# A graph layer's spilled edges summed in a free place of the last slot tile, and a re-ordered lead-in

## The chip, the cores and the metric

The kernel runs on one core of a Trainium2 chip. Its time is the device time of one execution in microseconds (us). The core has five engines with an instruction queue each: TensorE (PE, with its weight loads shown as PEld), VectorE (DVE), ScalarE (ACT), GpSimd (POOL) and SyncE (SP), which here only issues transfers. Each engine works through its instructions in the order in which they were written and waits at semaphores for the others.

## The reference, cut to what matters

```python
N, E, D = 6250, 100000, 128            # nodes, edges (sorted by dst), width
Xs  = x[src]
msg = where(edge_type == 0, Xs @ W_data.T + b_data, Xs @ W_control.T + b_control)
agg = segment_sum(msg, dst, N)
out = relu(agg + (x @ W_self.T + b_self))
return layernorm(x + out)              # over the 128 columns, eps 1e-5
```

Nodes are padded to 49 blocks of 128. Inputs and output are float32.

## The kernel before

**The table.** The message of an edge depends only on its source node and its type, so the kernel first computes one row for each of the 2 x 49 x 128 pairs. Each value is kept as three bfloat16 parts that add up to the float32 value, so a row has 3 x 128 columns. `multiply` computes a block of 128 nodes for both types on PE (`y`, lines 464 and 466), `take` copies a part to SBUF on ScalarE (`m`, line 475) and `leave` subtracts it again on PE (line 482), three parts in turn. All parts stay in SBUF (`m3`, 98 source tiles of 128 rows), and `store` also writes them to memory (`table`, line 492).

**Edges by destination block.** Edges are sorted by destination, so the edges of a block lie in a window of 18 x 128 edges. `starts` finds where the windows begin: an indirect load fetches 49 rows of edges (`er`), VectorE counts (`less`, `first_f`), PE turns the counts into one row (line 359), VectorE writes `first` (line 361), and SP then reads each start into a register and loads the window (`win`, line 376).

**Two ways to sum.** 40 blocks (the "p" blocks, eight groups of five) are summed with the table in SBUF. The other nine (the "g" blocks) fetch each edge's row from the table in memory by an indirect load on POOL (`msg`, line 845) and sum on PE (`agg_g`), in between the p blocks' work.

For a p block the edges are sorted into 98 buckets, one per source tile, of R = 32 places each:

- `edge_fields` (VectorE) splits the edges of a group into fields; `bucket_hots` compares them with the bucket numbers (`hot_st`, line 550).
- `ranks` gives each edge its place in its bucket, 18 steps a group: PE adds up `tri` times the hots (`acc`), VectorE takes the maximum (`slot`, line 567), PE adds `rest`. It is a chain between the two engines.
- `fill_a` and `fill_b` put the source row and the destination of each edge into its place (`two`, `v`, line 604).
- `fill_c` copies the result (`vs`), writes the source rows to memory (`packed`, line 622), turns the destinations into columns of four buckets each (`vd`, line 632; `to`, line 637), and lists the edges that found no place in their bucket, the spilled edges, at most 32 a group. Their positions in the list come from eight matmuls (lines 652 and 654), the list itself from a further eight (line 677), and POOL gathers their table rows (`msg_s`, line 694).
- `spread` loads `packed` to all 128 partitions (`rows`, line 718), `select` compares it with the partition number (line 725): a one-hot matrix that picks source rows.
- `gather` multiplies it with a source tile: 4 x 32 rows of messages, four buckets, a slot tile (`g_ps`, line 752). There are 25 slot tiles for 98 buckets; in the last one the buckets 96 and 97 fill half of the partitions, and its other two matmuls repeat bucket 97.
- `evict` copies the tile to SBUF as `gs` (line 761, ScalarE; in the last group VectorE too), `to_hots` builds the one-hot of destinations in two pieces per block (`hot_d`, line 739), and `add_up` multiplies the two into the block's sum `agg`. After the last tile one more set of matmuls adds the spilled edges (`msg_s` by `hot_s`). Row 32 of these tiles holds b_self and a row of ones, so that this also adds the bias; the g blocks have a pair of tiles for the bias alone (`msg_b`, `hot_b`).

Every sum is written as four matmuls of 32 output partitions each (`by_columns`, line 229):

```python
for c in range(0, P, 32):
    T.matmul(out[c : c + 32], lhsT[:, c : c + 32], rhs, **flags)
```

`own_of` adds `W_self x` to the sum in float32. `finish_blocks` adds the three parts (`whole`, line 150), applies relu and adds x; `normalise` does the layer norm for a whole group (root on ScalarE, `scale` on VectorE, one activation per block on ScalarE, line 187) and stores it. The group's sums use one PSUM buffer, so the next block's first sum waits for `whole`.

**The order.** All of these are Python generators of steps. A planner (`Order.run`) holds an assumed cost for each step and engine, a due time (`due`) and what the step needs, and picks which step comes next; the engines' instruction queues are written in that order. A changed cost or due time therefore moves instructions on every queue, and nothing else decides the order: the schedule isn't changed by the chip or the compiler.

Of the kernel before, what the change touches and what calls it, by code (L numbers as in the profile page):

```python
# [9 lines left out]
F32 = mybir.dt.float32  # L10
BF16 = mybir.dt.bfloat16
# [8 lines left out]
P = 128  # L20
# [23 lines left out]
NC = 4 * NS  # L44
XS = 4
RB = 3
M = 8
SLOT = 128.0
# [163 lines left out]
def sums_over_windows(ctx, tc, x, xt, edges, w, bias, table, packed, total,  # L212
# [42 lines left out]
    bias3 = const.tile([P, 2 * D], BF16, name="bias3")  # L255
# [16 lines left out]
    for i in range(3):  # L272
        A.copy(bias3[32 * i : 32 * i + 1, :], parts[0:1, i, : 2 * D])
# [6 lines left out]
    for j in range(RJ):  # L280
# [18 lines left out]
               for n in sorted({DC, CH, *GROUPS})}  # L299
# [3 lines left out]
    spill_tiles = [(const.tile([P, Q * P], BF16, name=f"hot_s{i}"),  # L303
                    const.tile([P, D3], BF16, name=f"msg_s{i}")) for i in range(2)]
    hot_b = const.tile([P, P], BF16, name="hot_b")
    msg_b = const.tile([P, D3], BF16, name="msg_b")
    slot_values = [const.tile([P, (Q + 1) // 2, NC], BF16, name=f"vs{i}") for i in range(2)]
    slot_b = {n: const.tile([P, R, n], BF16, name=f"slot{n}") for n in sorted({*GROUPS})}

    def constants():  # L310
# [13 lines left out]
        yield step("set2", {"V": 1.2})  # L324
# [3 lines left out]


        for vs in slot_values:  # L330
            V.memset(vs, 255.0)


        for i, (hot, msg) in enumerate([*spill_tiles, (hot_b, msg_b)]):
            yield step(("spill0", i), {"V": 1.6})
            V.memset(hot, 0.0)
            V.memset(hot[R : R + 1, :], 1.0)
            V.memset(msg, 0.0)
            V.tensor_copy(msg[R : R + 1, :].rearrange("p (i c) -> p i c", i=3),
                          parts[0:1, :, 2 * D :])  # L340
# [7 lines left out]
    def starts():  # L348
        yield step("er", {"S": 0.0}, lag=10.0)
# [12 lines left out]
        for b in [*range(STARTS[2]), *range(NPB, NB), *range(STARTS[2], NPB)]:  # L362
            grp = [g for g in range(NPG) if STARTS[g] <= b][-1] if b < NPB else NPG
            free = [("fields", grp - 2)] if 1 < grp < NPG else []
            yield step(("win", b), {"S": 0.84}, "first", *free, lag=2.0)
# [26 lines left out]
    def due(kind, *i):  # L392
        if kind in ("p", "g") and i[0] in ("root", "rooted", "scale", "apply", "out"):
            n = i[1] + 1
            return BUILT + 10 + (BLOCK * sum(GROUPS[:n]) if kind == "p" else PACE * KT * GQ * n)
# [15 lines left out]
        if kind in ("set2", "spill0"):  # L411
            return 40.0
# [3 lines left out]
        if kind == "table":  # L416
            return LEAD + each * (at_part[i[0]] + PARTS[i[0]]) + 6
# [39 lines left out]
    def multiply():  # L457
        for i, (g, b, n) in enumerate(two_blocks):
            for j in range(n):
# [6 lines left out]
                T.matmul(y[:, j, :], ones_b, bias3, start=False, stop=True, skip_group_check=True)  # L466
# [35 lines left out]
    places, spills, rows = {}, {}, {}  # L502
# [38 lines left out]
    def bucket_hots():  # L541
        chunks = [(grp, c) for grp in range(NPG) for c in range(KT // KC)]
        for i, (grp, c) in enumerate(chunks):
            n = GROUPS[grp]
            free = [("v", chunks[i - HB][0], chunks[i - HB][1] * KC + KC - 1)] if i >= HB else ["set"]
            yield step(("hot", grp, c), {"V": 0.13 + KC * NT * n / 1920}, ("fields", grp), ("counts", n), *free)
# [26 lines left out]
    def fill_a():  # L573
        for grp, n in enumerate(GROUPS):
            for c in range(KT // KC):
                yield step(("two", grp, c), {"V": 0.4 + 0.3 * n}, ("rank", grp, c * KC + KC - 1), ("slots", n),
# [32 lines left out]
    def fill_c():  # L609
        for grp, n in enumerate(GROUPS):  # L610
# [6 lines left out]
            A.copy(vs[:, : n // 2, :NT], vt[:, : n // 2, :])  # L617
            if n % 2:
                A.copy(vs[: 2 * R, n // 2, :NT], vt[: 2 * R, n // 2, :])
            yield step(("packed", grp), {"S": 0.4}, ("vs", grp), lag=2.5)  # L620
            for i in range(2):
                nc.sync.dma_start(
                    packed[b0 + i : b0 + n : 2, :].rearrange("j (r s) -> r j s", r=R),
                    vs[2 * R * i : 2 * R * i + R, : (n + 1 - i) // 2, :NT],
# [4 lines left out]
            for q in range(n):  # L629
                c0 = (q % 2 * 2 + 1) * R  # L630
                for t in range(4):
                    T.matmul(vd_v[t * R : (t + 1) * R, q, :], ident_b[:, c0 : c0 + R],
                             vs[:, q // 2, t::4], start=True, stop=True, skip_group_check=True)
            free = [("d", STARTS[grp - 1] - 1, (NS - 1) // DC)] if grp > 1 else []
            yield step(("to", grp), {"A": 0.3}, ("vd", grp), *free)
            to = work.tile([P, Q, NS], BF16, name="to")
            A.copy(to[:, :n, :], vd_v)
# [4 lines left out]
            yield step(("over", grp), {"V": 0.7}, ("rank", grp, KT - 1), ("to", grp))  # L642
# [5 lines left out]
            flags = work.tile([P, M], BF16, name="flags", bufs=1)  # L648
            V.tensor_single_scalar(flags, last, 0.0, op=ALU.is_gt)
            yield step(("pos", grp), {"T": 0.6}, ("over", grp), ("to", grp))  # L650
            pos = ps_a.tile([P, 512], F32, name="small")
            T.matmul(pos[:, :M], tri, flags, start=True, stop=False, skip_group_check=True)
            for c in range(M - 1):
                T.matmul(pos[:, c + 1 : M], ones_b,
                         flags[:, c : c + 1].to_broadcast([P, M - 1 - c]),
                         start=False, stop=c == M - 2, skip_group_check=True)
# [13 lines left out]
            V.tensor_copy(pos_sb, pos[:, :M])  # L670
# [5 lines left out]
            for c in range(M):  # L676
                T.matmul(listed[:R, :4], hs[:, c, :], f4[:, c, :], start=c == 0, stop=c == M - 1,
                         skip_group_check=True)
            free = [("sum", STARTS[grp - 1] - 1)] if grp > 1 else []
# [11 lines left out]
            hot_s, msg_s = spills[grp] = spill_tiles[grp % 2]  # L691
            V.tensor_scalar(hot_s[:R, : n * P], iota_f[:R, : n * P], dq, None, op0=ALU.is_equal)
            yield step(("spilled", grp), {"G": 0.8}, ("listed", grp), *stored, lag=2.5)
            G.indirect_dma_start(  # L694
                out=msg_s[:R], out_offset=None, in_=table[:, :],
# [25 lines left out]
    def select():  # L721

        for b in range(NPB):
            yield step(("sel", b), {"V": 1.2}, ("rows", b))
            V.tensor_scalar(rows[b], rows[b], pid1, None, op0=ALU.is_equal)  # L725

    def to_hots():
        tiles = [(b, c) for b in range(NPB) for c in range(-(-NS // DC))]
        for i, (b, c) in enumerate(tiles):
# [6 lines left out]
            yield step(("d", b, c), {"V": 0.13 + P * n / 1920}, ("to", grp), "built", ("counts", DC), *free)  # L736
# [8 lines left out]
    def gather():  # L745
        for i, (b, g) in enumerate(tiles):
# [3 lines left out]
            for t in range(4):  # L750
                s = min(4 * g + t, NT - 1)
# [3 lines left out]
    def evict():  # L755
        for i, (b, g) in enumerate(tiles):
            free = [("s", *tiles[i - EB])] if i >= EB else []
            costs = {"A": 0.37, "V": 0.53} if b >= STARTS[-1] else {"A": 0.37}
            e = yield step(("e", b, g), costs, ("g", b, g), *free)
            gs_tiles[b, g] = gs = late.tile([P, D3], BF16, name="gs", bufs=EB)  # L760
            (A.copy if e == "A" else V.tensor_copy)(gs, g_tiles.pop((b, g))[:, :D3])  # L761
# [274 lines left out]
```

## Time and profile before

| | us |
|---|---|
| median of three runs | 639.49 (637.23 to 640.24) |
| the profiled execution | 641.69 |
| its span, first to last instruction | 639.9 |
| first gather on PE (`g_ps`) | starts at 94.10 |
| last sum on PE (`agg<-msg_s`) | starts at 627.12 |
| last store (`out`) issued | 632.79 |

The profiled execution is the one that all views below describe; it took 1.8 us more than its span and 2.2 us more than the median. Up to about 94 us lies the lead-in (table, windows, the first group's sorting); from 94 to 627 us the blocks are summed; the rest is the end. In a row of busy times by stretch the columns are: stretch and its length, busy time and instructions of PE, PEld, DVE, ACT and POOL, the granted clock of TensorE (1.00 is full), the share of the DMA engines and GB/s. In a row of the timeline they are: start, duration, engine, line, operation, output and inputs, shapes and count; in brackets the idle time of the engine ahead of it and what ended that. Durations of matmuls overlap, because they are pipelined; their starts tell how fast they follow one another.

### The profile page before, as it was taken

How to read it: one execution, taken by the hardware profiler on the slowest of the kernel's cores; microseconds unless marked ns; L12 is line 12 of the kernel's file. 1: busy time of each engine (PE TensorE's matmuls, PEld its weight loads, DVE VectorE, ACT ScalarE, POOL GpSimd, SP SyncE). 2: the span in 40 equal slices, each digit the busy share in tenths (PEclk: the TensorE clock that was granted, in tenths of full speed). 3: DMA queues.
4: the chain of work that ended last, by engine and by line, in shares of the span. 5: the costliest groups of instructions: out<-in, count | busy, mean ns of one | idle time of the engine just before them, and what ended most of it. 6: DMA issues, size and time to landing. Idle time of an engine off the chain costs nothing.

```text
span 639.9 us, 28774 instructions
## 1 busy us (share of the span) xinstructions
PE 581.3 (91%) x12337; PEld 490.8 (77%) x12337; DVE 465.0 (73%) x1005; ACT 467.2 (73%) x1127; POOL 195.0 (30%) x178
## 2 busy tenths in 40 slices
PE   5689968999999999999999998999899999999992
PEld 3435537888878887988789887988798789887891
DVE  6555577866986689858987698768785876658783
ACT  6635535777887778788778798877788787878782
POOL 1000005323434342435333343233243533343200
PEclk9979979999999999999999999999899999999997
DMA  3655572512443153324341434234331543145200
GB/s 102 190 167 158 152 245 104 155 45 92 161 121 97 46 198 117 101 55 153 124 143 52 146 112 127 91 99 153 112 96 39 171 150 101 44 140 180 76 18 27
DMA packets 57550, 74.56 MB, mean 117 GB/s; under 512 B 14592, under 2 KB 48779, under 8 KB 57415
## 3 DMA queue, kind: packets, MB, share of 16 engines
q1 hardware_dynamic: 48149, 52.99, 25.9%
q0 software_dynamic: 8112, 16.25, 8.9%
q10 hardware_dynamic: 1154, 3.41, 1.7%
q8 instruction: 98, 1.61, 1.0%
q14 instruction: 37, 0.30, 0.2%
HBM read 59.54 MB, written 13.08 MB: 113 GB/s over the span
## 4 chain that ended last, share of the span: by engine, by line
PE 73%; DVE 10%; DMA 5%; ACT 5%; issue 4%; SPq 1%; POOL 1%; ACTq 0%; DVEq 0%; POOLq 0%
PE agg L229 26%; PE g_ps L752 24%; PE acc L229 8%; PE small L604 7%; PE agg_g L229 4%; ACT gs L761 3%; PE y L464 2%; DVE hot_st L550 2%; DVE slot L567 2%; DMA msg<-table,idx 2%; DVE two L588 2%; DMA xt<-in_xt 1%; PE y L482 1%; DMA rows<-packed 1%; DVE hr L583 1%
## 5 line engine op out<-in xcount | busy, mean ns | idle before, releaser
L761 ACT CAST gs<-g_ps 128x384 bf16<-128x384 f32 x961 | 396.9, 500 | 115.8 <-PE g_ps L752 89.3
L752 PE MATMUL g_ps<-m,rows 128*32 128x384 bf16 x4000 | 370.3, 331 | 5.9 <-issue 2.2
L229 PE MATMUL agg<-gs,hot_d 128*32 128x384 bf16 x4000 | 359.6, 335 | 15.9 <-ACT gs L761 12.3
L845 POOL DMA_INDIRECT msg<-table,idx x162 | 185.2, 1143 | 295.3 <-PE agg_g L229 146.2
L229 PEld LDWEIGHTS <-hot_d 128*32 128x32 bf16 x4000 | 225.0, 137 | 43.3 <-issue 33.0
L752 PEld LDWEIGHTS <-rows 128*32 128x32 bf16 x4000 | 211.4, 137 | 24.3 <-issue 14.7
L567 DVE TENSOR_REDUCE slot<-acc 128x5 bf16<-128x490 f32 x144 | 95.5, 663 | 76.9 <-PE acc L229 55.9
L739 DVE TENSOR_TENSOR hot_d<-count,to 128x1664 bf16<-128x1664 bf16 x80 | 84.9, 1068 | 13.4 <-PE agg L229 8.4
L604 PE MATMUL small<-hot_st,two 128*32 128x98 bf16 x1440 | 80.5, 291 | 1.4 <-issue 0.7
L229 PE MATMUL acc<-hot_st,rest 128*32 128x490 bf16 x544 | 64.4, 382 | 10.8 <-DVE slot L567 9.6
L229 PE MATMUL acc<-hot_st,tri 128*32 128x490 bf16 x576 | 68.6, 383 | 3.0 <-DVE hot_st L550 2.7
L229 PE MATMUL agg_g<-msg,hot_g 128*32 128x384 bf16 x648 | 69.7, 330 | 1.4 <-DMA msg<-table,idx 1.2
L604 PEld LDWEIGHTS <-two 128*32 128x32 bf16 x1440 | 64.8, 117 | 7.1 <-issue 3.1
L475 ACT CAST m<-y 128x512 bf16<-128x512 f32 (+1 forms) x75 | 40.5, 580 | 37.7 <-PE y L466 19.2
L550 DVE TENSOR_TENSOR hot_st<-count,st_b 128x2940 bf16<-128x2940 bf16 x24 | 47.7, 1993 | 16.2 <-PE small L604 9.1
L725 DVE TENSOR_SCALAR rows<-rows,pid 128x3136 bf16<-128x3136 bf16 x40 | 41.5, 1039 | 3.7 <-DMA rows<-packed 3.3
L229 PEld LDWEIGHTS <-rest 128*32 128x32 bf16 x544 | 24.5, 97 | 20.0 <-issue 18.7
L694 POOL DMA_INDIRECT msg_s<-table,row_i x8 | 7.5, 942 | 104.2 <-DVE most L701 89.8
L464 PE MATMUL y<-w_sb,xt 128*128 128x256 f32 x98 | 35.1, 448 | 1.7 <-DMA xt<-in_xt 1.7
L229 PEld LDWEIGHTS <-hot_g 128*32 128x32 bf16 x648 | 33.7, 124 | 3.1 <-issue 1.5
L150 DVE TENSOR_REDUCE whole<-agg 128x128 f32<-128x384 f32 x40 | 22.2, 554 | 17.4 <-PE g_ps L752 11.5
L229 PEld LDWEIGHTS <-tri 128*32 128x32 bf16 x576 | 25.0, 100 | 5.8 <-issue 5.4
(141 smaller groups left out, 403.1 us busy)
## 6 DMA issues: line engine op xcount, KB each, us to landing
rows<-packed SPq DMA_DIRECT2D x40, 784.0 KB
table<-m SPq DMA_DIRECT2D x10, 768.0 KB
msg<-table,idx POOLq DMA_INDIRECT x162
xt<-in_xt ACTq DMA_DIRECT2D x5, 512.0 KB
xt_p<-in_xt SPq DMA_DIRECT2D x40, 64.0 KB
xs_p<-in_x SPq DMA_DIRECT2D x40, 64.0 KB
out<-h_p SPq DMA_DIRECT2D x8, 320.0 KB
win<-in_edges SPq DMA_DIRECT2D x40, 27.0 KB
```

Of the source, the lines that this page charges most:

```text
L150: nc.vector.tensor_reduce(whole, agg.rearrange("p (i c) -> p c i", i=3), axis=AX.X, op=ALU.add)
L229: T.matmul(out[c : c + 32], lhsT[:, c : c + 32], rhs, **flags)
L464: T.matmul(y[:, j, :], xts[g][:, b + j - at_part[g], :], w_sb[:, : 2 * D], start=j == 0, stop=False, skip_group_check=True)
L475: A.copy(part_of(b, n, i), ys[b][:, :n, :].rearrange("p b (t c) -> p t b c", t=2))
L550: V.tensor_tensor(hot, counted[n][:, None, 1 : NT + 1, :].to_broadcast([P, KC, NT, n]), fields[grp][2][:, c * KC : c * KC + KC, None, :].t ...
L567: V.tensor_reduce(slots[grp][:, k, :], by_q, axis=AX.X, op=ALU.max)
L604: T.matmul(vt[c0 : c0 + R, q // 2, :], two[:, k % KC, i, :, q], hot[:, k % KC, :, q], start=k == 0 and q < 2, stop=k == KT - 1, skip_group ...
L725: V.tensor_scalar(rows[b], rows[b], pid1, None, op0=ALU.is_equal)
L739: V.tensor_tensor(hot, counted[DC][:, :, :n], places[grp][:, q, None, c * DC : c * DC + n].to_broadcast([P, P, n]), op=ALU.is_equal)
L752: T.matmul(g_ps[t * R : (t + 1) * R, :D3], rows[b][:, :, s], m3[:, s, :], start=True, stop=True)
L761: (A.copy if e == "A" else V.tensor_copy)(gs, g_tiles.pop((b, g))[:, :D3])
L845: G.indirect_dma_start(out=msgs[j, k], out_offset=None, in_=table[:, :], in_offset=bass.IndirectOffsetOnAxis(ap=idx[:, j, k : k + 1], axis=0),
```

## The change

1. The spilled edges move into the last slot tile. The two buckets of that tile now fill its upper 64 partitions, and the list of up to 32 spilled edges the lowest 32: POOL gathers into `mixed[:32]`, `evict` copies 64 partitions of the last tile into `mixed[64:]`, and one sum takes both. The extra sum with `msg_s`, `hot_s` goes, and so do the constants for it. For this the buckets are numbered anew (`BUCKETS`, `PLACES`: consecutive buckets stand under each other), the last gather tile has two matmuls instead of four, `to` becomes two fixed tiles that are filled by two copies, and VectorE writes the spilled edges' destinations into `to` (so `hot_d`'s second piece waits for the list).
2. b_self is added beside `W_self x`, by four matmuls of 128 columns for each block (`ones_b` with three rows of `bias3`); the g blocks' `msg_b`, `hot_b` go.
3. The positions in the spill list come from one matmul over the number of spilled edges per partition, and a few small VectorE instructions.
4. The last group is normalised in two pieces: four blocks, then the last one alone.
5. Costs, delays and due times of the planner are changed: several VectorE steps cost more, table writes are due 8 us later, the windows are given longer to land, and the g blocks' index step (`far_g`, `idx`) waits for the table's block 36.

```diff
+IN_LAST = NT - 4 * (NS - 1)
+PLACES = [NS - (t < 4 - IN_LAST) for t in range(4)]
+BUCKETS = [sum(PLACES[:t]) for t in range(4)]
...
-    for i in range(3):
-        A.copy(bias3[32 * i : 32 * i + 1, :], parts[0:1, i, : 2 * D])
+    for i in range(3):
+        A.copy(bias3[32 * i : 32 * i + 1, :], parts[0:1, i, :])
...
-        for i, (hot, msg) in enumerate([*spill_tiles, (hot_b, msg_b)]):
-            yield step(("spill0", i), {"V": 1.6})
-            V.memset(hot, 0.0)
-            V.memset(hot[R : R + 1, :], 1.0)
-            V.memset(msg, 0.0)
-            V.tensor_copy(msg[R : R + 1, :].rearrange("p (i c) -> p i c", i=3),
-                          parts[0:1, :, 2 * D :])
+        for to in to_bufs:
+            V.memset(to, NONE)
+        for tile_n in mixed:
+            V.memset(tile_n, 0.0)
...
-        yield step("er", {"S": 0.0}, lag=10.0)
+        yield step("er", {"S": 0.0}, lag=9.0)
...
-            yield step(("win", b), {"S": 0.84}, "first", *free, lag=2.0)
+            yield step(("win", b), {"S": 0.84}, "first", *free, lag=3.0 if grp < NPG else 6.0)
...
-            return LEAD + each * (at_part[i[0]] + PARTS[i[0]]) + 6
+            return LEAD + each * (at_part[i[0]] + PARTS[i[0]]) + 14
...
-            yield step(("to", grp), {"A": 0.3}, ("vd", grp), *free)
-            to = work.tile([P, Q, NS], BF16, name="to")
-            A.copy(to[:, :n, :], vd_v)
+            yield step(("to", grp), {"A": 0.5}, ("vd", grp), "set2", *free)
+            to = to_bufs[grp % 2]
+            A.copy(to[:, :n, : NS - 1], vd_v[:, :, : NS - 1])
+            A.copy(to[2 * R :, :n, NS - 1], vd_v[2 * R :, :, NS - 1])
...
-            T.matmul(pos[:, :M], tri, flags, start=True, stop=False, skip_group_check=True)
-            for c in range(M - 1):
-                T.matmul(pos[:, c + 1 : M], ones_b,
-                         flags[:, c : c + 1].to_broadcast([P, M - 1 - c]),
-                         start=False, stop=c == M - 2, skip_group_check=True)
+            T.matmul(pos[:, :1], tri, number_b, start=True, stop=True, skip_group_check=True)
...
-            V.tensor_copy(pos_sb, pos[:, :M])
+            V.scalar_tensor_tensor(start, number, -SLOT, pos[:, :1], op0=ALU.mult, op1=ALU.add)
+            V.scalar_tensor_tensor(pos_sb, slot_f[:, :M], start, flags, op0=ALU.add, op1=ALU.mult)
...
-            hot_s, msg_s = spills[grp] = spill_tiles[grp % 2]
-            V.tensor_scalar(hot_s[:R, : n * P], iota_f[:R, : n * P], dq, None, op0=ALU.is_equal)
+            V.tensor_scalar_add(to[:R, :n, NS - 1], place_q[:R, :n], dq)
             yield step(("spilled", grp), {"G": 0.8}, ("listed", grp), *stored, lag=2.5)
             G.indirect_dma_start(
-                out=msg_s[:R], out_offset=None, in_=table[:, :],
+                out=mixed[grp % 2][:R], out_offset=None, in_=table[:, :],
...
-            gs_tiles[b, g] = gs = late.tile([P, D3], BF16, name="gs", bufs=EB)
-            (A.copy if e == "A" else V.tensor_copy)(gs, g_tiles.pop((b, g))[:, :D3])
+            if g < NS - 1:
+                gs, at = late.tile([P, D3], BF16, name="gs", bufs=EB), slice(P)
+            else:
+                gs, at = mixed[blocks[b][0] % 2], slice(2 * R, P)
+            gs_tiles[b, g] = gs
+            (A.copy if e == "A" else V.tensor_copy)(gs[at], g_tiles.pop((b, g))[at, :D3])
...
-            if g == NS - 1:
-                hot_s, msg_s = spills[grp]
-                by_columns(aggs[b], hot_s[:, q * P : (q + 1) * P], msg_s, start=False, stop=True,
-                           skip_group_check=True)
...
-            if b >= NPB:
-                by_columns(aggs[b], hot_b, msg_b, start=False, stop=False, skip_group_check=True)
+            by_columns(aggs[b][:, :D], ones_b, bias3[:, 2 * D :], start=False, stop=False,
+                       skip_group_check=True)
...
+    PIECES = [(g, 0, n) for g, n in enumerate(GROUPS[:-1])]
+    PIECES += [(NPG - 1, 0, GROUPS[-1] - 1), (NPG - 1, GROUPS[-1] - 1, 1)]
...
-        yield step("idx", {"V": 1.5}, *[("win", b) for b in range(NPB, NB)])
+        yield step("idx", {"V": 1.8}, ("y", NB * 3 // 4), *[("win", b) for b in range(NPB, NB)])
```

The planner's costs for `hot_st` and `hot_d` go from elements / 1920 to elements / 1580, for `two` from 0.3 to 0.365 a block, for the position step from 0.6 to 0.15 on PE, and for `select` from 1.2 to 1.05.

## The prediction

> **What bounds the kernel now.** I read the page first (shares, slices, chain), then busy times by stretch, then the lead-in, the end of a block and the end of the kernel in the timeline.
>
> ```profile
> span 639.9 us, 28774 instructions
> PE 581.3 (91%) x12337; PEld 490.8 (77%) x12337; DVE 465.0 (73%) x1005; ACT 467.2 (73%) x1127; POOL 195.0 (30%) x178
> ...
> PE   5689968999999999999999998999899999999992
> ...
> PEclk9979979999999999999999999999899999999997
> ```
>
> TensorE is the busiest engine and is full from the eighth slice on; the digits fall only in the lead-in and at the very end. The busy time by stretch (PE, PEld, DVE, ACT, POOL, clock, DMA) says what each stage is limited by:
>
> ```profile
> 25.00:33.00 8.00, 2.78 (x24) 1.59 (x22) 7.86 (x14) 2.13 (x5) 0.00 (x0) 1.00 0.73 207
> 33.00:36.40 3.40, 3.40 (x18) 1.48 (x15) 2.22 (x10) 1.63 (x3) 0.00 (x0) 0.50 0.61 197
> 36.50:43.20 6.70, 3.90 (x32) 1.99 (x32) 2.43 (x9) 2.04 (x4) 0.00 (x0) 1.00 0.41 120
> 43.30:46.60 3.30, 3.30 (x16) 1.30 (x16) 1.40 (x3) 1.18 (x3) 0.00 (x0) 0.50 0.95 291
> 47.00:83.00 36.00, 35.17 (x409) 20.58 (x407) 19.58 (x26) 18.93 (x34) 0.00 (x0) 1.00 0.53 163
> 98.00:627.00 529.00, 503.96 (x11632) 446.06 (x11621) 404.11 (x855) 416.13 (x1031) 191.85 (x169) 1.00 0.35 108
> ```
>
> From 25 to 47 us PE waits for VectorE's rank chain and runs twice at half clock; from 47 on PE is the limit. The chain of waits, cut to 98 to 627 us, lies on PE for 80% (agg 31.3, g_ps 28.9, acc 8.4, small 6.9, agg_g 4.7). So work taken from PE there counts at about 0.8.
>
> **The lead-in.** These are VectorE's and SP's rows:
>
> ```profile
> 15.19 0.41 SPq L492 DMA_DIRECT2D table<-m  x1
> 16.38 4.00 SPq L376 DMA_DIRECT2D win<-in_edges  x5
> ...
> 23.36 0.32 DVE L517 TENSOR_TENSOR rel_b<-win,base 128x90 bf16<-128x90 int32 x1 [9.39 <-DMA win<-in_edges]
> ...
> 31.51 0.66 DVE L567 TENSOR_REDUCE slot<-acc 128x5 bf16<-128x490 f32 x1
> ...
> 36.15 0.67 DVE L567 TENSOR_REDUCE slot<-acc 128x5 bf16<-128x490 f32 x1 [1.11 <-PE acc L229]
> 39.84 0.27 DVE L832 TENSOR_SCALAR far_g<-win_g 128x162 int32<-128x162 int32 x1 [3.02 <-DMA win_g<-in_edges]
> ...
> 41.35 0.08 DVE L837 DVE_READ_ACCUMULATOR low_g<-rel_g,low_g 128x1 f32 x1
> ```
>
> The windows are queued behind a table write that waits for ScalarE until 15.19, though `first` was ready at 13.97 (13.77 + 0.20). Then VectorE stops 3.02 us at `far_g` for the gathered blocks' windows, with the next `slot` queued behind it and PE's next `rest` and `tri` behind that.
>
> By the instruction order of the changed kernel: (a) `first` on PE follows five y blocks and one pair of leaves instead of six and two: 13.49 falls to about 12.7 (the skipped pair starts at 12.63). The memsets ahead of `less` shrink, so VectorE doesn't hold it. (b) SP issues the five windows before any table write: from about 14.2 (12.7, `first` 0.3, register load and rest 1.2) against 16.38, so -2.2; with the same 4.0 us of issue and 3.1 us of landing `rel_b` starts near 21.2. The table writes that they pass move 4.4 us later; their reader, POOL, first gathers at 96.8. (c) But group 1's fields now precede the first `slot`: 21.2 + 2.4 + 5.8 (three `hot_st`) + 2.3 = 31.7, against 31.51: nothing gained there yet. (d) The second `slot` no longer stands behind those fields: 31.51 to 34.38 becomes about 1.8, -1.1. (e) `far_g` goes behind block 36's y, so 36.15 to 41.35 (5.2) becomes one slot step of 1.8: -3.4. (f) Without that stall the half clock of 43.30 to 46.60 should go: -0.5 to -1.6. Its own 1.5 us of VectorE work returns in the stretch 47 to 83, where VectorE is busy 19.58 of 36; if PE weren't the limit there, it would cost up to 1.5. I take -5.0; bounds -2 (PE now waits some 3.4 us ahead of the first `slot` and may fall to half clock then; part of `far_g` returns) and -7.
>
> The Trainium skill ("TensorE: Matmul & The Clock Gate", Part 1) puts the fall to half clock behind an idle window of about 3.4 us. Here waits of only about 3 us (`far_g` 3.02) precede both 0.50 rows, so they count already. By the rule alone (f) would be nothing, and the lead-in -4.5.
>
> After `vs` come the `packed` write (4.03 us in the chain) and the first `rows` load (5.19), unchanged. The second `rows` load now passes the last table write on SP: the table lands perhaps 2 us later, and POOL's first gathers with it. They are issued at 98.0 and first used at 104.9, which covers about 2 us net of a landing of 2.5. Uncovered, it would cost that once.
>
> **The block stage.** The end of a block, and the position step, on PE:
>
> ```profile
> 608.81 0.39 PE L229 MATMUL agg<-gs,hot_d 128*32 128x384 bf16 x4
> 608.98 0.39 PE L229 MATMUL agg<-msg_s,hot_s 128*32 128x384 bf16 x4
> 609.14 1.41 PE L752 MATMUL g_ps<-m,rows 128*32 128x384 bf16 x20
> ...
> 360.42 0.18 PE L652 MATMUL small<-flags,tri 128*128 128x8 bf16 x1
> 360.46 0.31 PE L654 MATMUL small<-flags,ones_b 128*128 128x7 bf16 x7
> 360.70 0.39 PE L752 MATMUL g_ps<-m,rows 128*32 128x384 bf16 x4
> ```
>
> Starts are read, since durations overlap: four column matmuls of 384 take 0.163 us.
> - Spill wave gone: 40 x 0.163 = -6.5. It is the last sum ahead of `whole`, with nothing beside it.
> - The gathered blocks' bias wave of 384 gone: 9 x 0.163 = -1.5.
> - b_self: 49 new waves of four with 128 columns. By columns 0.163 x 128/384 = 0.054; the nearest row with small tiles, `small<-vs,ident_b`, starts 20 matmuls between 84.07 and 84.21, well under 0.05 per four. So 0.06 x 49 = +2.9. The skill (same page, Part 3) says that LDWEIGHTS overlaps matmuls in flight only where the row group differs, and here all use all rows: at 32 columns / 1.2 GHz that would add 4 x 0.027, 0.16 in all, +7.9 as an estimate. The 0.163 of a 384 wave, with four loads of 137 ns each, leaves no room for it, so I use +2.9 and keep +5.4 (four loads in series) for the range.
> - Positions: seven matmuls fewer at 0.025 (0.28 us between 360.42 and 360.70): 8 x 7 x 0.025 = -1.4. The remaining one keeps the change of tiling: the 0.32 us ahead of 360.42 stays.
> - The last gather tile has two matmuls instead of four, side by side before too: 0.
>
> PE: -6.5 on the sum; times 0.8, -5.2. Beside it: ScalarE gets one more small copy a group (8 x about 0.24, as the 64-row `vs` copy, 1.9 us) under 416 of 529 busy; VectorE gets four small instructions of some 0.15 and loses `hot_s` of 0.56 a group: level. If that cover were gone, +2. The table's second half of destinations now waits for the spill list; the list is done near the POOL gathers (159.1 for group 1), and the group's first last-tile sum is at 182.9: 20 us of room, and no new wait. New costs in the planner for VectorE's steps also shuffle the order; PE's waits for ScalarE's copies, 12.3 us in 31 waits at present, may go either way: 0, bounds -5 and +4.
>
> **The end.**
>
> ```profile
> 630.73 2.03 ACT L187 ACTIVATE h_p<-h_p,shift,rstd 128x128 f32<-128x128 f32 x5 [1.29 <-DVE shift L181]
> ...
> 632.79 0.39 SPq L194 DMA_DIRECT2D out<-h_p  x1
> ```
>
> One activation instead of five: 2.03 to 0.49, -1.5. The store shrinks from 320 to 64 KB; at the 261 GB/s of 634 to 635 us that is -1.0. The other four blocks' root, scale and activations (1.2 us VectorE, 1.9 ScalarE) now fall into the last block's copies, which both engines share there: +0.5. Together -2.0 (bounds -0.5 and -2.6).
>
> **Sum.** -5.0 - 5.2 - 2.0 = -12.2. The profiled execution took 641.69 (span 639.9), so it becomes 629.5; it ran 2.2 above the median of 639.49, from which I get 627.3.
>
> **Rivals.**
> 1. ScalarE and VectorE take over (chance 0.16). For: both are over 75% busy from 98 to 627, and in the bursts of five gather tiles PE starts only every 0.37 us, at ScalarE's pace. Against: 80% of the chain is PE. Block stage -1, total -8: 631.5.
> 2. The lead-in gives nothing (0.12): group 1's windows land later than 29.3 and hold the first `slot`, or PE's wait before it costs a half-clock stretch. Against: they are issued by about 23. Total -7.2: 632.3.
> 3. The shuffled order helps (0.14): with truer costs PE's waits fall by 5 and the lead-in gives 6.5: about 621.
> 4. Slower (0.05): the shuffled order puts ScalarE's bursts (five `h_p` activations, 2.0 us) where PE's lead of four tiles (four `g_ps` buffers, 4 x 0.33 = 1.3 us) is spent, block after block. PE's longest wait for ScalarE is 1.7 us now. From 0.31 us of added wait in each of 40 blocks on it eats the 12.2; at 0.45 the time is 645.
> The change doing nothing at all is ruled out by the instruction counts (272 fewer on PE).
>
> **Chances and range.** The forecast itself has 0.53 and holds 623 to 631. With the rivals 619 to 635.5 leaves out about 2 in 10. A measurement here tells 0.5% (3.2 us) from no change; 636.3 is missed only by rival 4 and by 1 or 2 with two bounds gone wrong: faster 0.90, same 0.06, slower 0.04.
>
> **What would show it.** Right: no `agg<-msg_s`; `small` with one position matmul; `rel_b` near 21, no wait at `far_g`, `packed` issued near 79 instead of 83.7; no 0.50 row near 43; from the first `g_ps` to the last `agg` 528 instead of 533; `out` issued 1.5 us after `shift`, and the end about 6 us after it. Wrong: `packed` not before 83; waits of PE for `gs` above 20 us; bias waves spaced by 0.15 or more; or a last block longer than 8.6 us.

## The result, and the profile after

The changed kernel took 632.21 us (median of four runs, 631.18 to 635.54), the kernel before beside it 639.87: 7.7 us less where 12.2 were forecast. The ratio over the single runs is 0.990 (95% interval 0.985 to 0.994, which is 3.6 to 9.6 us); the quotient of the medians is 0.988, because one of the four runs, 635.54, had a granted clock of 0.936 where the other three had 0.984 to 0.987. The profiled execution spans 629.5 us against 639.9; the kernel before's was 1.8 us above its median, so the spans lie 10.4 apart.

The page of the changed kernel (span, busy time, the slices of PE and of its clock):

```profile
span 629.5 us, 28502 instructions
...
PE 576.5 (92%) x12201; PEld 476.0 (76%) x12201; DVE 461.8 (73%) x1024; ACT 473.5 (75%) x1141; POOL 193.7 (31%) x178
...
PE   5899879998999999999899999999999999999992
...
PEclk9989979999999999999999999999999999999997
```

PE has 136 matmuls less and is full one slice sooner. The busy time by stretch (PE, PEld, DVE, ACT, POOL, clock, DMA):

```profile
31.40:34.80 3.40, 3.40 (x23) 1.10 (x16) 0.69 (x2) 1.17 (x2) 0.00 (x0) 0.51 0.80 250
35.00:47.00 12.00, 12.00 (x141) 6.56 (x139) 6.11 (x10) 6.31 (x11) 0.00 (x0) 1.00 0.59 168
47.00:73.00 26.00, 25.86 (x287) 14.79 (x291) 17.16 (x26) 14.88 (x27) 0.00 (x0) 1.00 0.72 221
83.00:617.50 534.50, 507.32 (x11546) 435.80 (x11544) 408.22 (x887) 425.57 (x1053) 191.40 (x170) 1.00 0.35 111
```

From 35 to 73 us PE hardly stands still, and up to 47 us one half-clock stretch of 3.4 us is left where there were two. The lead-in on SP:

```profile
13.18 3.76 SPq L372 DMA_DIRECT2D win<-in_edges  x5
17.04 0.94 SPq L488 DMA_DIRECT2D table<-m  x2
...
74.18 0.80 SPq L618 DMA_DIRECT2D packed<-vs  x2
```

The same write in the chain of the kernel before:

```profile
83.70 4.03 DMA packed<-vs
```

VectorE after the change:

```profile
18.66 0.31 DVE L513 TENSOR_TENSOR rel_b<-win,base 128x90 bf16<-128x90 int32 x1 [6.21 <-DMA win<-in_edges]
...
29.11 0.67 DVE L563 TENSOR_REDUCE slot<-acc 128x5 bf16<-128x490 f32 x1
30.47 0.67 DVE L563 TENSOR_REDUCE slot<-acc 128x5 bf16<-128x490 f32 x1 [0.70 <-PE acc L232]
...
55.35 0.26 DVE L841 TENSOR_SCALAR far_g<-win_g 128x162 int32<-128x162 int32 x1
```

The windows go out ahead of the table writes, the first `slot` starts 2.4 us sooner than before, and `far_g` waits for nothing at 55.35. `packed` is written at 74.18 instead of 83.70. PE's first steps of the rank chain, before and then after:

```profile
27.83 0.39 PE L229 MATMUL acc<-hot_st,tri 128*32 128x490 bf16 x4 [2.72 <-DVE hot_st L550]
```

```profile
24.79 0.39 PE L232 MATMUL acc<-hot_st,tri 128*32 128x490 bf16 x4
...
29.83 0.39 PE L232 MATMUL acc<-hot_st,rest 128*32 128x490 bf16 x4 [2.31 <-DVE slot L563]
```

PE no longer waits ahead of the first `tri`. The end, in the timeline of all engines:

```profile
617.51 0.39 PE L232 MATMUL agg<-mixed,hot_d 128*32 128x384 bf16 x4
...
620.81 0.16 DVE L184 SCALAR_TENSOR_TENSOR shift<-mv_p,rstd 128x1 f32<-128x1 f32 x1
...
621.00 0.49 ACT L190 ACTIVATE h_p<-h_p,shift,rstd 128x128 f32<-128x128 f32 x1 [1.20 <-DVE shift L184]
621.06 0.14 DVE L922 CAST total<-total_f 1x1 int32<-1x1 f32 x1
621.52 0.34 SPq L197 DMA_DIRECT2D out<-h_p  x1
```

One activation instead of five; `out` goes out 0.7 us after `shift` instead of 2.3, but the execution ends 8.0 us after `out`, where it was 7.1.

Cut at the first `g_ps` and at the last `agg` of a p block, this and every later run divide so. The three sets of experiments ran on three chips, and each set has its own runs of the kernel before; medians are compared within a set only. The ratios are taken over the single runs and differ from the quotient of the medians by up to 0.003. The three columns of stages are of one execution each.

| run | lead-in (first `g_ps`) | block stage | last sum to end | median | ratio to before (95%) |
|---|---|---|---|---|---|
| before | 94.1 | 533.1 | 12.7 | 639.87 | |
| after | 83.4 | 534.1 | 12.0 | 632.21 | 0.990 (0.985-0.994) |
| set 1: e1 lead-in figures alone | 87.3 | 502.8 | 12.8 | 604.89 | 0.994 (0.991-0.996) |
| e2 before, no spill sum | 93.0 | 493.1 | 12.9 | 602.32 | 0.988 (0.985-0.992) |
| e3 after, old block costs | 86.9 | 500.6 | 12.0 | 599.66 | 0.985 (0.981-0.988) |
| e4 after, no b_self | 83.1 | 495.8 | 11.9 | 592.57 | 0.972 (0.969-0.975) |
| set 2: e5 before | 94.2 | 499.0 | 12.8 | 607.28 | |
| e6 after | 82.0 | 499.4 | 12.0 | 595.74 | 0.980 (0.976-0.983) |
| e7 after, one more sum | 81.9 | 500.6 | 11.9 | 596.81 | 0.982 (0.979-0.985) |
| e8 before, last block alone | 94.0 | 498.0 | 12.0 | 605.96 | 0.998 (0.995-1.000) |
| set 3: e9 after | 82.2 | 533.5 | 12.0 | 627.95 | 0.987 (0.985-0.990) |
| e10 after, narrow copies | 83.4 | 524.5 | 12.0 | 620.86 | 0.977 (0.974-0.979) |
| e11 after, seven ahead | 83.2 | 529.2 | 12.0 | 624.07 | 0.982 (0.979-0.984) |
| e12 after, VectorE helps | 83.0 | 526.2 | 11.9 | 621.79 | 0.978 (0.975-0.981) |

The kernel before took 607.88, 607.28 and 635.48 us in the three sets. So nearly all of the gain was in the lead-in (-10.7 in the first pair of profiles, -12.2 in set 2, where -5.0 was forecast), and the block stage, where -5.2 was forecast, gained nothing (+1.0 and +0.4). The experiments ask why.

### The profile page after: what moved, and what is told of

Same layout as the page of the kernel before. It is cut to its first block, busy times and chain, and to the rows that moved or that the text cites. A ratio compares the mean times of both kernels' runs of the same rounds, so it can differ in the third digit from the quotient of the medians.

```text
span 629.5 us, 28502 instructions
## 1 busy us (share of the span) xinstructions
PE 576.5 (92%) x12201; PEld 476.0 (76%) x12201; DVE 461.8 (73%) x1024; ACT 473.5 (75%) x1141; POOL 193.7 (31%) x178
## 3 DMA queue, kind: packets, MB, share of 16 engines
q10 hardware_dynamic: 1154, 3.41, 1.7%
## 4 chain that ended last, share of the span: by engine, by line
PE 79%; DVE 7%; ACT 6%; DMA 4%; issue 3%; SPq 1%; POOL 0%; another core or an unknown queue 0%; ACTq 0%; DVEq 0%; POOLq 0%
PE agg L232 27%; PE g_ps L754 26%; PE acc L232 10%; PE small L600 7%; PE agg_g L232 4%; ACT gs L769 4%; PE y L460 2%; DVE slot L563 2%; DMA rows<-packed 2%; PE y L478 1%; ACT h_p L190 1%; DVE two L584 1%; DVE hot_st L546 1%; ACT m L471 1%; DMA msg<-table,idx 1%
## 5 line engine op out<-in xcount | busy, mean ns | idle before, releaser
L769 ACT CAST gs<-g_ps 128x384 bf16<-128x384 f32 x928 | 382.3, 497 | 109.7 <-PE g_ps L754 79.2
L232 PE MATMUL agg<-gs,hot_d 128*32 128x384 bf16 x3840 | 347.5, 335 | 12.7 <-ACT gs L769 9.6
L232 PEld LDWEIGHTS <-hot_d 128*32 128x32 bf16 x4000 | 231.8, 137 | 42.3 <-issue 31.4
L754 PEld LDWEIGHTS <-rows 128*32 128x32 bf16 x3920 | 218.0, 138 | 33.2 <-issue 24.9
L232 PE MATMUL agg_g<-msg,hot_g 128*32 128x384 bf16 x648 | 67.8, 329 | 1.2 <-DMA msg<-table,idx 0.8
L694 POOL DMA_INDIRECT mixed<-table,row_i x8 | 7.7, 958 | 103.9 <-PE g_ps L754 81.8
L460 PE MATMUL y<-w_sb,xt 128*128 128x256 f32 x98 | 32.4, 420 | 1.8 <-DMA xt<-in_xt 1.8
```

The lines of the kernel that those rows point to most:

```text
L460: T.matmul(y[:, j, :], xts[g][:, b + j - at_part[g], :], w_sb[:, : 2 * D], start=j == 0, stop=False, skip_group_check=True)
L754: T.matmul(g_ps[t * R : (t + 1) * R, :D3], rows[b][:, :, s], m3[:, s, :], start=True, stop=True)
L769: (A.copy if e == "A" else V.tensor_copy)(gs[at], g_tiles.pop((b, g))[at, :D3])
```

## The experiments

### Where the lead-in's gain comes from: e1, e3

e1 puts the new planner figures of the lead-in alone into the kernel before:

```diff
-        yield step("er", {"S": 0.0}, lag=10.0)
+        yield step("er", {"S": 0.0}, lag=9.0)
...
-            yield step(("win", b), {"S": 0.84}, "first", *free, lag=2.0)
+            yield step(("win", b), {"S": 0.84}, "first", *free, lag=3.0 if grp < NPG else 6.0)
...
-            return LEAD + each * (at_part[i[0]] + PARTS[i[0]]) + 6
+            return LEAD + each * (at_part[i[0]] + PARTS[i[0]]) + 14
...
-        yield step("idx", {"V": 1.5}, *[("win", b) ...
+        yield step("idx", {"V": 1.8}, ("y", NB * 3 // 4), *[("win", b) ...
```

> The kernel before with the planner figures of the lead-in alone (latency of the first gather and of the windows, due time of the table writes, fields of the gathered blocks behind y 36). Between the two profiles the first g_ps moved from 94.10 to 83.39 (-10.7) where -5 was forecast. Theory A, the figures alone do it: first g_ps near 84, total 9 to 11 us below before (about 630), because the block stage stays at 533. Rival B, half of it came with the smaller memsets and the other edits: first g_ps near 89, total about 5 us below before.

e3 takes the changed kernel and puts back the old planner costs of the block stage, and with them those of `hot_st` and `two`, which the lead-in uses too (of each changed line the cost alone is shown):

```diff
-{"V": 0.13 + KC * NT * n / 1580}            # hot_st
+{"V": 0.13 + KC * NT * n / 1920}
-{"V": 0.4 + 0.365 * n}                      # two
+{"V": 0.4 + 0.3 * n}
-{"V": 1.05}                                 # select
+{"V": 1.2}
-{"V": 0.13 + P * n / 1580}                  # hot_d
+{"V": 0.13 + P * n / 1920}
-{"T": 0.165}                                # sums
+{"T": 0.165 if g < NS - 1 else 0.33}
-{"T": 0.5}                                  # own rows
+{"T": 0.45 if b < NPB else 0.62}
```

> The changed kernel with the planner's costs of the block stage put back to those of before (hot_st, two, select, hot_d, the last sum at 0.33, own rows at 0.45 and 0.62); the lead-in figures and all of the work stay. Theory A, the new order of the block stage put in the waits (+6.5 us of gaps between the profiles): the stage falls from 534 to 528 to 530, total 4 to 6 us below the changed kernel, about 627. Rival C, pace: stage 533 to 535, total within 2 us of the changed kernel (632).

The first `g_ps` in the timeline of PE, of e1, then e3, then e6 (the changed kernel whole):

```profile
87.35 1.50 PE L752 MATMUL g_ps<-m,rows 128*32 128x384 bf16 x16 [1.55 <-DVE rows L725]
```

```profile
86.86 1.50 PE L754 MATMUL g_ps<-m,rows 128*32 128x384 bf16 x16 [1.80 <-DVE rows L725]
```

```profile
82.01 1.50 PE L754 MATMUL g_ps<-m,rows 128*32 128x384 bf16 x16 [0.53 <-DVE rows L725]
```

Set 1 alone can be added up, because e2 has the lead-in of the kernel before and e4 that of the changed one: from e2's 93.0 the figures of the lead-in give -5.6 (-6.9 from e5's 94.2, of another chip), the other edits at old costs 0.5 more, and the new costs of VectorE's steps another 3.8 (4.9 against e6, which has no half-clock stretch in the lead-in before 47 us, where e3 has one). Neither theory on e1 held: its first `g_ps` lies between the two. For e3, theory A fell: the old costs don't shorten the block stage (500.6), and what they lose they lose in the lead-in.

e1's total fell by only 3.0 us in the medians (2.2 to 5.5 by the interval), less than its lead-in. Its stage begins at half clock, from 87.3 to 93.1 (granted clock 0.51), where that of e5, of another chip, has 94.2 to 97.4 (0.55): 2.6 us more at half speed, some 1.3 us. The other 2.5 us of its longer stage are spread over waits and were not followed.

### What PE's time is worth in the block stage: e2, e4, e7

Three kernels keep the order of the instructions and change PE's work alone. e2, from the kernel before (with `msg_s` goes the b_self that its row 32 holds):

```diff
-                       start=g == 0, stop=False, skip_group_check=True)
-            if g == NS - 1:
-                hot_s, msg_s = spills[grp]
-                by_columns(aggs[b], hot_s[:, q * P : (q + 1) * P], msg_s, start=False, stop=True,
-                           skip_group_check=True)
+                       start=g == 0, stop=g == NS - 1, skip_group_check=True)
```

> The kernel before without the spilled edges' sum (left out: the 160 matmuls agg<-msg_s of 40 blocks, so the spilled edges are missing from the result); the order of everything else is kept. Theory A, TensorE's time counts at 0.8 in the block stage as forecast: 5.2 us below before (6.5 x 0.8), stage 528. Rival C, the stage runs at the pace of ScalarE's copies and TensorE's time is mostly cover: 0 to 2 us below before, the gaps on PE over 300 ns (72 us) growing by 5 or more.

e4, from the changed kernel:

```diff
-            by_columns(aggs[b][:, :D], ones_b, bias3[:, 2 * D :], start=False, stop=False,
-                       skip_group_check=True)
```

> The changed kernel without b_self (left out: the 49 bias waves agg<-bias,ones_b and agg_g<-bias,ones_b, 196 matmuls, which take 3.58 + 0.85 us start to start in its trace); the order of everything else is kept. Theory A: 3.5 to 4.4 us below the changed kernel, about 628. Rival C, pace: 0 to 1.5 us below it, 631 to 632.

e7, from the changed kernel, with `nothing` a tile of zeros:

```diff
...
-                       start=g == 0, stop=g == NS - 1, skip_group_check=True)
+                       start=g == 0, stop=False, skip_group_check=True)
+            if g == NS - 1:
+                by_columns(aggs[b], d_hots[b, g // DC][:, :, g % DC], nothing, start=False, stop=True,
+                           skip_group_check=True)
```

> The changed kernel with a 26th sum at the end of each block (hot_d of the last tile by a tile of zeros: 160 matmuls more, at the place where the spilled edges' sum stood); the order of everything else is kept. Theory A, TensorE's time counts whole at this place: 5 to 6.5 us above the changed kernel. Theory C, the boundary of two blocks runs at ScalarE's pace and covers it: 0 to 2 us above.

Beside e7 ran the two kernels whole:

> The kernel before once more, for a trace of it from the chip of this set: on the chip of the first set it took 608 us where it took 640 in the first profile. All theories: the durations of one instruction are the same (ScalarE's copies every 0.375 us, a wave of four matmuls in 0.163), and what differs are the gaps on PE between g_ps, the copy and agg. On a chip with short hand-overs the block stage is near 500 us, on one with long ones near 533.

> The changed kernel once more, beside the kernel before on the same chip as the two that follow. Theory A, order: lead-in -10, block stage 0 to +2, end -0.7: 8 to 11 us below before. Theory C, pace of ScalarE: the same lead-in, and the block stage 0 to -2 on a chip with short hand-overs. The time from a block's last sum to the first sum of the next was 1.85 us on average before and 2.07 after in the first two profiles (39 times, +8.8 us); if the order causes it, it is 0.15 to 0.25 longer here too.

e2 is 5.6 us below before in the medians (7.0 by the ratio), and its stage 5.9 below that of e5: in the old order the spilled edges' sum was worth what the forecast put on it. e4 is at 0.972 of before and the changed kernel (e6) at 0.980; their stages differ by 3.6 us, for 4.1 us of bias waves: these too count nearly whole. Theory A, then, twice. Both comparisons of stages cross from set 1 to set 2, whose kernels before took 607.88 and 607.28. But e7, which puts 160 matmuls back where the spilled edges' sum stood, costs 1.1 us in all (the single runs of the two overlap) and 1.2 in the stage. There theory C holds.

The place decides. Of the stage's differences, e4's 3.6 us lie inside the blocks, from a block's first sum to its last, and none at the 39 block ends; e7's 1.2 lie at the block ends and none inside. Of e2's 5.9, 4.1 lie at the ends and 1.7 inside, where e8, with the same work there as e5, differs from e5 by 1.0.

The time from one start on PE to the next, summed over the block stage by the kind that starts (worked out from the starts in the three traces of set 2), shows what covers it:

| us, start to start | e5 before | e6 after | e7 one more sum |
|---|---|---|---|
| `g_ps` | 171.7 | 179.6 | 172.1 |
| of it, gaps over 0.3 us | 10.9 | 22.1 | 13.5 |
| `agg` from gather tiles | 173.9 | 171.5 | 172.7 |
| spilled edges' sum, or zeros | 6.7 | 0 | 6.9 |
| bias waves (before: `msg_b`) | 0.9 | 4.1 | 4.1 |
| positions of the list | 3.4 | 2.0 | 2.0 |
| all other | 142.4 | 142.2 | 142.8 |

Taking the sum away put 7.9 us on `g_ps`, putting it back took 7.5 off. The place can be looked at. PE and then ScalarE in e6, from the last sum of a block to the first sum of the next:

```profile
252.27 0.40 PE L232 MATMUL agg<-mixed,hot_d 128*32 128x384 bf16 x4
252.43 0.40 PE L754 MATMUL g_ps<-m,rows 128*32 128x384 bf16 x4
252.59 0.44 PE L232 MATMUL acc<-hot_st,rest 128*32 128x490 bf16 x4
252.80 1.05 PE L754 MATMUL g_ps<-m,rows 128*32 128x384 bf16 x12
253.62 0.39 PE L232 MATMUL agg_g<-msg,hot_g 128*32 128x384 bf16 x4
253.84 0.39 PE L754 MATMUL g_ps<-m,rows 128*32 128x384 bf16 x4
254.00 0.88 PE L232 MATMUL agg<-gs,hot_d 128*32 128x384 bf16 x16
```

```profile
251.66 0.47 ACT L769 CAST mixed<-g_ps 64x384 bf16<-64x384 f32 x1
252.16 2.78 ACT L769 CAST gs<-g_ps 128x384 bf16<-128x384 f32 x7
```

The same place in e7:

```profile
253.17 0.39 PE L232 MATMUL agg<-mixed,hot_d 128*32 128x384 bf16 x4
253.33 0.39 PE L232 MATMUL agg<-nothing,hot_d 128*32 128x384 bf16 x4
253.50 0.39 PE L756 MATMUL g_ps<-m,rows 128*32 128x384 bf16 x4
253.66 0.44 PE L232 MATMUL acc<-hot_st,rest 128*32 128x490 bf16 x4
253.87 0.88 PE L756 MATMUL g_ps<-m,rows 128*32 128x384 bf16 x12
254.52 0.39 PE L232 MATMUL agg_g<-msg,hot_g 128*32 128x384 bf16 x4
254.74 0.39 PE L756 MATMUL g_ps<-m,rows 128*32 128x384 bf16 x4
254.91 0.88 PE L232 MATMUL agg<-gs,hot_d 128*32 128x384 bf16 x16
```

```profile
252.57 0.47 ACT L771 CAST mixed<-g_ps 64x384 bf16<-64x384 f32 x1
253.07 2.78 ACT L771 CAST gs<-g_ps 128x384 bf16<-128x384 f32 x7
```

With the extra sum or without it, the next block's first sum starts 1.73 or 1.74 us after the `mixed` sum. ScalarE copies without a pause in both, seven tiles in 2.78 us, and with four `g_ps` buffers a gather tile can't start before the copy of the fourth tile before it is done. That the waits are spread over the gather waves (three of them fill 0.82 us in e6, 0.65 in e7, for 0.49 of work) is why the view of waits shows so little of it: each is shorter than the 0.4 us that a wave stays busy.

Two chains meet at a block's end: last sum, `whole` on VectorE, first sum; and ScalarE's next copies. In e5 the first sum started over 0.4 us after `whole` had ended at 17 of 39 block ends, in e6 at 35 of 39. By this count `whole`, and with it the spilled edges' sum, still set the pace at about half of the block ends before, and after, the copies do at nearly all. e7 bears out the second half: at those 35 ends the added sum cost 0.02 us on average, at the other four 0.10. The first half is rougher: without the sum (e2) the 22 ends became 0.12 us shorter, but the 17 others too, by 0.09.

### Are the copies the limit there: e10, e11, e12

> The changed kernel once more, beside the three that follow: 0.980 of before on a chip with short hand-overs (596 against 607), 0.990 on one with long ones.

e10 makes the copies at this place shorter and keeps the order (for that it gives out the `gs` buffers by number):

```diff
...
-            (A.copy if e == "A" else V.tensor_copy)(gs[at], g_tiles.pop((b, g))[at, :D3])
+            wide = D if b and g < 4 else D3
+            (A.copy if e == "A" else V.tensor_copy)(gs[at, :wide], g_tiles.pop((b, g))[at, :wide])
```

> The changed kernel with the copies of the first four gather tiles of blocks 1 to 39 cut to 128 of 384 columns (left out: the other two thirds of these tiles' messages), the order kept. Theory C, ScalarE's copies set the pace from the last sum of a block to the first sum of the next: a copy every 0.2 instead of 0.375 us takes 0.4 to 0.7 us from a block, so the mean time between these sums falls from 1.89 to about 1.5 and the total by 10 to 20 us. Theory A, TensorE or VectorE's whole sets it: total 0 to 3 us below the changed kernel.

The mean time between the two sums (from the last matmul of a block's last sum to the first of the next block's) fell from 2.06 in e9 to 1.74 us, and the total by 7.1. Theory C's sign and place are right, its size was too large: 39 x 0.32 = 12.5 us were taken from the block ends, and some came back elsewhere: 3.4 inside the blocks (PE's gaps over 0.3 us ahead of `agg<-gs` grew from 27.5 to 31.1) and 1.3 in the lead-in. ScalarE and PE at one block end of e10:

```profile
557.99 0.47 ACT L774 CAST mixed<-g_ps 64x384 bf16<-64x384 f32 x1
558.49 1.00 ACT L774 CAST gs<-g_ps 128x128 bf16<-128x128 f32 x4
559.70 0.86 ACT L774 CAST gs<-g_ps 128x384 bf16<-128x384 f32 x2 [0.20 <-PE g_ps L754]
```

```profile
558.51 0.39 PE L232 MATMUL agg<-mixed,hot_d 128*32 128x384 bf16 x4
...
559.00 0.77 PE L754 MATMUL g_ps<-m,rows 128*32 128x384 bf16 x12
559.60 0.88 PE L232 MATMUL agg<-gs,hot_d 128*32 128x384 bf16 x16
```

Now ScalarE waits for PE, the three gather waves follow each other at 0.2 us, and the first sum comes 1.09 us after the last.

e11 lets PE go to the first sum sooner, e12 lets VectorE take some of the copies:

```diff
             free = [("e", *tiles[i - GB])] if i >= GB else ["built"]
+            if g == 7:
+                free.append(("s", b, 0))
```

> The changed kernel with at most seven gather tiles of a block ahead of its first sum (8 or more in 27 of 40 blocks now), all work kept. Theory C: each gather wave less in the burst takes 0.2 to 0.37 us from the boundary, and costs 0.16 later where TensorE is the limit: 2 to 6 us below the changed kernel. Theory A or a late whole: TensorE stands at the first sum instead of at the gather wave, 0 to 4 us above it.

```diff
-            costs = {"A": 0.37, "V": 0.53} if b >= STARTS[-1] else {"A": 0.37}
+            costs = {"A": 0.37, "V": 0.53} if b >= STARTS[-1] else {"A": 0.37, "V": 0.56} if b and g < 4 else {"A": 0.37}
```

> The changed kernel with VectorE allowed to copy any of the first four gather tiles of a block where the planner finds it sooner (17 copies more on VectorE, 0.56 us each), all work kept. Theory C: 17 boundaries shorter by one copy of 0.375: 3 to 6 us below the changed kernel. Rival: VectorE takes whole and slot later for it, 0 to 4 us above.

Both edits let the planner move other instructions too. e11 is 3.9 us below the changed kernel: the mean time between the two sums fell from 2.06 to 1.71, 13.5 us in all, and 9.2 came back inside the blocks. e12 is 6.2 below it and 13.7 below the kernel before: 0.978 of that, where the changed kernel has 0.987. It keeps all of the work and is the fastest version of set 3 that does. From its page:

```profile
L769 ACT CAST gs<-g_ps 128x384 bf16<-128x384 f32 x906 | 374.6, 497 | 108.9 <-PE g_ps L754 83.6
...
L769 DVE CAST gs<-g_ps 128x384 bf16<-128x384 f32 x54 | 29.6, 555 | 25.7 <-PE g_ps L754 12.4
```

The block ends are hardly shorter in e12 (2.01 us against 2.06 in e9), other than expected; more gather waves fit into them (202 waves of four over the 39 block ends, against 191 in e9), and PE's gaps over 0.3 us ahead of `g_ps` fell from 30.4 to 19.9 us. Of its 7.3 us in the stage, 5.2 lie inside the blocks. So the proof that the copies set the pace at the block ends is e10, not e12.

### The end: e8

e8 gives the kernel before the pieces of the changed one, the last block's norm on its own:

```diff
+    PIECES = [(g, 0, n) for g, n in enumerate(GROUPS[:-1])]
+    PIECES += [(NPG - 1, 0, GROUPS[-1] - 1), (NPG - 1, GROUPS[-1] - 1, 1)]
...
```

> The kernel before with the last block normalised alone and nothing else. By the forecast 2.0 us below before. By the two profiles, where the time from the last sum to the end fell from 12.7 to 12.0, 0.7 below: the end then holds a floor that the smaller activation and store don't touch.

It is 1.3 us below before in the medians (ratio 0.998, 0.995 to 1.000, so hardly told from nothing), and the time from the last sum to the end fell from 12.8 to 12.0, as between the first two profiles. The whole of the end's gain belongs to this edit, and it is 0.8.

## Why the forecast came near, point by point

The time was within the range of 619 to 635.5, but outside the 623 to 631 that the forecast itself held, and in set 2 the gain was even the forecast's (607.28 to 595.74, -11.5 in the medians; -12.7 in the spans). That is luck: the terms were not right, and two errors of about 6 us each, one in the lead-in and one in the block stage, cancelled.

- **Lead-in, -5.0 forecast, -10.7 and -12.2 found.** The mechanism was right: `far_g` without a wait, windows ahead of the table writes. The sizes were not. Step (b): windows issued at 13.18, not 14.2, and `rel_b` started 1.7 us after the last issue instead of 3.0, at 18.66 and not near 21.2. Step (c), "nothing gained there yet", failed with it: the first `slot` came 2.4 us sooner. And PE's wait of 2.72 us ahead of the first `tri` (27.83 before) is gone, because `tri` now stands among the y blocks, at 24.79; the working had no term for it. Three waits of PE, 2.72, 2.50 and 2.80, became one of 2.31. Behind `packed` another 1.2 us went, where the working had "unchanged": the write and the first `rows` load took 3.47 and 4.57 us in the chain instead of 4.03 and 5.19.
- **Planner order, forecast as 0.** e3 against e4: the new costs of VectorE's steps bring 3.8 us of the lead-in. A sum over the moved steps of part 5 alone could not contain them; the order of the instructions was there to be read.
- **Step (f), half clock, -0.5 to -1.6.** In the first profile after, one stretch of 3.4 us is left before 47 us (31.4 to 34.8), as in e4 and e10; in e6, e7, e9, e11 and e12 there is none. From `rel_b` to the first `g_ps` the three runs with it took 64.6 to 65.1 us and the five without 62.8 to 63.6. So a stretch is worth about 1.5 us, within the bounds.
- **Block stage, -5.2 forecast, +1.0 and +0.4 found.** The step that failed is the first term: "It is the last sum ahead of `whole`, with nothing beside it." ScalarE's next copies stood beside it. In the old order taking it away gave 5.9 (e2); in the new one its place is covered (e7, 1.2 for 6.9 of work). With that the stage of set 2 adds up, as an estimate: -1.2 for the sum, +3.6 for b_self (e4), -0.9 for the gathered blocks' bias and -1.4 for the positions (both start to start) make +0.1, and +0.4 was found. What in the new order shifts the balance is not settled: with old costs for the planner (e3, of another chip) the block ends are 2.7 us shorter in all than in e6, but the blocks 3.9 longer.
- **b_self, 0.06 a wave.** The trace has 3.58 us for the 40 waves, 0.09 each, and set 2 0.08: 4.1 to 4.4 us with the g blocks instead of 2.9. The Trainium skill ("TensorE: Matmul & The Clock Gate", Part 3), by which LDWEIGHTS overlaps only where the row group differs, would have given 0.16 by the prediction's estimate. The trace has about half of that, and more than the 0.06 of the working; what fills the rest was not tested.
- **Positions, -1.4.** 3.4 to 2.0 us: as forecast.
- **The end, -2.0 forecast, -0.7 and -0.8 found.** The activations gave their 1.6 us (`out` 0.7 after `shift` instead of 2.3). The store's -1.0 failed: from `out` to the end is 8.0 us instead of 7.1, though the smaller store's packets are over somewhat sooner. So another chain ends there. `total`, the count on which the program branches, is written at 621.06, 8.4 us before the end (8.5 in e8, 9.1 in the kernel before), right behind `shift` on VectorE. That this branch sets the end was not tried.
- **The rivals.** The first one named the right mechanism for the block stage, "ScalarE and VectorE take over", with a stage of -1, and gave it 0.16. Its total, 631.5, lies nearer to 632.21 than the forecast's 627.3, but the lead-in brought twice what it took over from the forecast. Rival 2's total, 632.3, lies nearest of all, and its mechanism is refuted: the lead-in gave most. A total does not tell which mechanism is at work. The long waits of rival 4 were not seen: PE's longest wait for `gs` fell from 1.7 to 1.1 us.
- **Named as signs of a wrong forecast:** waits for `gs` over 20 us (9.6 + 2.7 found), bias waves spaced 0.15 (0.09), a last block over 8.6 us. None came, though the stage's term failed: the signs looked for long waits, and the time went into many short ones.

## What to carry to other kernels

An instruction on the busiest engine is worth what the place where it stands lets through: ask which other chain ends just after it, and if that one runs without a pause, price the removal near nothing, however full the engine is. A hand-written planner's cost figures are part of a change like any other edit, and moved more here than the matmuls did. Where PE is fed through a few buffers, sum the starts, not the waits: waits shorter than a matmul's own duration don't show as idle.

## What the hardware showed that was not expected

**The same program was 5% apart between sets of runs.** The kernel before took 640 us in the first pair of runs (its chip is not on record), and 608, 607 and 635 in the three sets, each on a chip of its own. Single instructions lasted the same (ScalarE's copies 500 ns in the first profile, 499 in e5; a wave of four column matmuls 0.16 us), the lead-in and the end too (94.1 and 94.2; 12.7 and 12.8). The whole difference lies in the block stage, 533.1 against 499.0, in PE's gaps over 0.3 us: 72.2 against 33.6 us. PE's waits for ScalarE's copies, before and e5:

```profile
PE agg L229 <- ACT gs L761: 12.3, 31, 1.7
```

```profile
PE agg L229 <- ACT gs L761: 4.4, 7, 1.2
```

What makes the passing of work from engine to engine slow is open; with one set on each chip, the chip and the time of the set can't be told apart. It matters for the change: in the slower runs it gained 7.7 and 7.5 us, in the faster 11.5. By an estimate the stage grew by some 4 us in the first pair: lead-in and end gave 10.7 + 0.7 between the first two profiles, and the medians gained 7.7.

**Half clock after short waits.** A stretch at 0.50 followed a wait of PE of 2.26 us (e10), 2.31 (first profile after) and 3.74 (e1), and none followed 2.21 (e6), 2.40 (e9) and 2.66 (e11). So the length of one wait does not decide. In the lead-ins of all traces the stretches lasted 3.41, 6.83 or 10.24 us, one, two or three times the same length. That fits the free-running window of which the Trainium skill tells ("TensorE: Matmul & The Clock Gate", Part 1), but not its full idle window of 3.4 us as the condition: 2.26 was enough once.
